# A hybrid attention kernel: squares of u behind the additions to k, weights read back in 256 KB parts, copies at the end moved

## The chip, the cores and the metric

The kernel runs on one core of a Trainium2 chip, in float32. The time is that of the device from start to end of one execution, in microseconds (us), as the median of several runs. A profile of one execution shows what each engine did: TensorE (PE, with its weight loads as PEld), VectorE (DVE), ScalarE (ACT), GpSimd (POOL), and SyncE (SP), which here issues DMAs.

## The reference, cut to what matters

Four layers with residuals over x of shape (2, 2048, 256): a gated scan, a feed-forward layer (FFN), an attention without softmax, and the FFN once more.

```
x = x + scan(layernorm(x));   x = x + ffn(layernorm(x))
x = x + hla(layernorm(x));    x = x + ffn(layernorm(x))

ffn(x): h = gelu(x @ ternary(W1).T + b1);  h @ ternary(W2).T + b2
hla(x), 16 heads of 64, step by step over t:
    G += k_t (k_t C);  S += k_t k_t^T;  C += q_t v_t^T
    o_t = q_t (S C - G)
    out @ W_o
```

The change lies in hla and in the way from it to the last FFN.

## The kernel before

**Attention in steps.** The 2048 positions of each of the two sequences are cut into 16 chunks of 128. A step `s` of the loop (L982, 32 steps, NS = 32) is one chunk `n = s // 2` of sequence `b = s % 2`; an even step is called `first` in the code. `more` is true while a further pair of chunks has still to be projected (s below 30). The chunk form of the recurrence needs, in each step: u = q S from the states before the chunk (`inter`, L835) plus the masked products of q and k inside the chunk (`products`, `intra`); the copy of u to SBUF (`evict`, L865, tile uT); the addition of k k^T to the states S and of u v^T to the states M (`update`, L874); and, one or two steps later, o = q M with the masked products of q and u, and the projection by W_o (`outward`, L899).

**The projections q, k, v** of a pair of chunks are done by seven products in place of eight (class `Seven`, L728). `go(i)` issues one product of PE and what follows it: a copy by ACT into the result (for 1, 5, 6, 4) or an addition by DVE (0, 3, 7). Products 1, 6, 7 and 4 share the PSUM bank X. So product 4 of k cannot start before the addition of product 7 has read that bank. In even steps k of the next pair is done, in odd steps q and v.

**Transposes through DRAM.** k and u are also needed transposed. DVE transposes squares of 32 x 32 into the tile sq (`turn_squares`, L914: skT for k by `keys_out`, suN for u by `units_out`), SP stores it to DRAM with one DMA of 512 KB (dkT, duN), then loads it in another order with four DMAs of 128 KB (`turn_rows`, L924: rkT, ruN), and ACT copies it to its place (`turn_end`, L935, tiles kT and uN; `units_end`, L948, for u). `update(s - 1, "uN", "vN", "M")` reads uN, `products(s, "kT", "p1")` reads kT. Only the last step's uN is made by PE (`units`, L952).

**PSUM.** Eight banks in three rings: four under "ps", two under "uT", two under "oT"; each request takes the next bank of its ring. The banks of `inter(s, "S", "uT")` are those of the ring "uT", and so is the bank X of k and of the last FFN's first products.

**Order.** PE, DVE, ACT and POOL run in the order in which the code issues their instructions (`manual_schedule`), so a line that is moved moves its instruction on its engine. SP issues DMAs in order too, and one that waits holds those behind it. DMAs issued by `nc.scalar.dma_start` stand in ACT's order.

**The last FFN.** Its weights, made ternary and combined for the seven products, were stored to DRAM by `ffn_weights_away` (w1 and w2 of 1 MB each, w1_s and w2_t3 of 768 KB each), since SBUF is needed for the attention. `ffn_weights_back` (L341) loads them into the room of wk and wv once these are read for the last time, by one DMA each:

```
            if s == NS - 4:
                last.weights("w1")
            elif s == NS - 3:
                last.weights("w2")
```

The class `Last` (L1129) does the first block of the last FFN beside the last two steps of the attention: `stats` and `rows` its norm, `turned` the transposes, `fill` the products of its first layer (generator `ffn_in`, with `apart=True`: the order p2, p1, p5, p6, p7, p3, p4 for each half), `out` those of its second. In the steps 30 and 31 `fill` stands where `k.go`, `q.go` and `v.go` stood before.

The functions that the change touches:

Of the kernel before, what the change touches and what calls it, by code (L numbers as in the profile page):

```python
# [17 lines left out]
FP = mybir.dt.float32  # L18
# [5 lines left out]
B, T, D = 2, 2048, 256  # L24
# [19 lines left out]
def kernel(  # L44
# [15 lines left out]
    nc = tc.nc  # L60
# [3 lines left out]
    const = ctx.enter_context(tc.tile_pool(name="const", bufs=1))  # L64
# [18 lines left out]
    wk = const.tile([P, ND, H * DK], FP, tag="wk", name="wk")  # L83
# [93 lines left out]
    def norm_rows(pool, cs, stats, xn=None, **kw):  # L177
        mv, rs, nb = stats
        if xn is None:
            xn = pool.tile([P, len(cs), D], FP, tag="xn", name=f"xn{cs[0]}", **kw)  # L180
        for c, g in enumerate(cs):
            if nb is None:
                nc.vector.tensor_scalar(
                    xn[:, c, :], x_sb[:, g, :], mv[:, c, 0:1], rs[:, c : c + 1],
                    ALU.subtract, ALU.mult,
                )
            else:
                nc.scalar.activation(  # L188
                    xn[:, c, :], x_sb[:, g, :], AF.Identity,
                    bias=nb[:, c : c + 1], scale=rs[:, c : c + 1],  # L190
                )
        return xn
# [145 lines left out]
            kept[nm] = dram.tile(w.shape, FP, tag=f"d{nm}", name=f"d{nm}")  # L338
            nc.sync.dma_start(out=kept[nm], in_=w)

    def ffn_weights_back(nm, tag):  # L341

        w = const.tile(kept[nm].shape, FP, tag=tag, name=f"{nm}_back")
        nc.scalar.dma_start(out=w, in_=kept[nm])
        return w

# [182 lines left out]
    def run(steps, n=None):  # L531
        for _ in steps if n is None else zip(range(n), steps):
            pass
# [169 lines left out]
    def attention(keep, pool, state, last):  # L703
# [241 lines left out]
        def units_out(s):  # L945
            turn_squares(s, "uN", d[s]["uT"].rearrange("f q (b i) -> f b q i", b=NQ))

        def units_end(s):  # L948
            turn_end(s, "uN")
            d[s]["uN"] = d[s]["uN"].rearrange("p a e -> p (a e)")  # L950
# [31 lines left out]
        for s in range(NS):  # L982
            first, n = s % 2 == 0, s // 2
            more = n + 1 < CPB
            inter(s, "S", "uT")
            products(s, "kT", "p1")
            if first and n + 2 < CPB:
                stats = norm_stats(norm_pool, pair(n + 2), bias=True)
            elif s == NS - 4:
                last.stats()  # L990
            elif s == NS - 2:
                last.second_stats()
            if s == 0:
                v.go(4)
                pairs[1] = norm_turned(norm_pool, pair(1), xn, bufs=1)
                pair_sums(1)
            if s % 2 == 1 and more:
                q, v = Seven(n + 1, "qT", "uT"), Seven(n + 1, "vN", "oT")
            if s == 1:
                q.go(2)  # L1000
                v.go(2)
                keys_out(s + 1)
            elif s % 2 == 1 and s + 1 < NS:
                keys_out(s + 1)
            if s == 2:
                k = Seven(n + 1, "kN", "uT")
                k.go(2)
            if first and s > 0:
                units_end(s - 1)
            if s >= 3:  # L1010
                outward(s - 3, 1)
            intra(s, "S", "kN", "p1", "uT")
            if s >= 2:
                intra(s - 2, "M", "vN", "p2", "oT")
            if s + 1 < NS:
                turn_rows(s + 1, "kT")
            evict(s, "uT")
            if not more:
                if s >= 2:
                    evict(s - 2, "oT")  # L1020
                last.begin(first)
                fill = last.fill
                fill(2)
                if not first:
                    units_end(s - 1)
                    units(s)
                fill(2)
            elif first:
                if s != 2:
                    k = Seven(n + 1, "kN", "uT")  # L1030
                    k.go(2)
                k.go(1)
                if s >= 2:
                    evict(s - 2, "oT")
                k.go(0, 5)
            else:
                if s >= 2:
                    evict(s - 2, "oT", dve)
                units_end(s - 1)
                units_out(s)  # L1040
                turn_rows(s, "uN")
                if s > 1:
                    q.go(2)
                    v.go(2)
                q.go(1)
                v.go(1)
                q.go(0, 5)
                v.go(0, 5)
                q.go(6)
                v.go(6)  # L1050
            if s == NS - 4:
                last.rows()
            elif s == NS - 1:
                last.second_rows()
            if s + 1 < NS:
                update(s + 1, "kN", "kN", "S")
            if s >= 1:
                update(s - 1, "uN", "vN", "M")
            if s == NS - 1:
                update(s, "uN", "vN", "M")  # L1060
            elif first:
                units_out(s)
            if not more:
                fill(2)
            elif first:
                k.go(6, 3, 7)
            else:
                v.go(7)
                q.go(7)
                v.go(3, 4)  # L1070
                q.go(3)
            if s + 1 < NS:
                turn_end(s + 1, "kT")
            if s >= 1:
                inter(s - 1, "M", "oT")
                products(s - 1, "uT", "p2")
            if not more:
                fill(1)
            elif first:
                k.go(4)  # L1080
                if n + 2 < CPB:
                    xn = norm_rows(norm_pool, pair(n + 2), stats)
            else:
                q.go(4)
            if not first and s + 2 < NS:
                keys_out(s + 2)
            if first:
                turn_rows(s, "uN")
            if not first and n + 2 < CPB:
                pairs[n + 2] = norm_turned(norm_pool, pair(n + 2), xn, bufs=1)  # L1090
                pair_sums(n + 2)
            elif s == NS - 3:
                last.turned()
            if s == NS - 4:
                last.weights("w1")
            elif s == NS - 3:
                last.weights("w2")
            if s >= 2:
                outward(s - 2, 0)
        last.out()  # L1100
# [16 lines left out]
    def pair(n):  # L1117
        return [b * CPB + n for b in range(B)]
# [10 lines left out]
    class Last:  # L1129
# [28 lines left out]
            self.rhs = ffn_rows(None, self.g0, xnT, [ts[:, i, :] for i in range(4)])  # L1158
            ffn_bias(self.g0)

        def weights(self, nm):
            nonlocal w1, w1_s, w2, w2_t3
            if nm == "w1":
                w1, w1_s = ffn_weights_back("w1", "wk"), ffn_weights_back("w1_s", "wk_t")
            else:
                w2, w2_t3 = ffn_weights_back("w2", "wv"), ffn_weights_back("w2_t3", "wv_t")

        def begin(self, first):
            if first:
# [110 lines left out]
```

## Time and profile before

| | us |
|---|---|
| median of 3 runs | 1244.42 (1243.24 to 1245.93) |
| the profiled execution: its time | 1245.38 |
| its span, first to last instruction | 1243.6 |
| PE busy | 1220.3 |
| DVE busy | 751.0 |
| ACT busy | 587.8 |
| POOL busy | 217.3 |

The attention runs from about 311 to 1053 us of the span. A line of a wait table reads: the engine and what it was about to do, the releaser, then the total in us, how often, and the longest. A line of the timeline reads: start, length, engine, line, operation, out<-in with shapes and count, and in brackets the idle time before it and what ended that. A line of the windows has the stretch, its length, the busy time of PE, PEld, DVE, ACT and POOL with counts of instructions, the clock granted to PE, the busy share of the 16 DMA engines, and GB/s. "Issue" is time in which an engine waited for nothing that the profile shows. ACTq and SPq are DMA issues in the order of ACT and SP.

### The profile page before, as it was taken

How to read it: one execution, taken by the hardware profiler on the slowest of the kernel's cores; microseconds unless marked ns; L12 is line 12 of the kernel's file. 1: busy time of each engine (PE TensorE's matmuls, PEld its weight loads, DVE VectorE, ACT ScalarE, POOL GpSimd, SP SyncE). 2: the span in 40 equal slices, each digit the busy share in tenths (PEclk: the TensorE clock that was granted, in tenths of full speed). 3: DMA queues.
4: the chain of work that ended last, by engine and by line, in shares of the span. 5: the costliest groups of instructions: out<-in, count | busy, mean ns of one | idle time of the engine just before them, and what ended most of it. 6: DMA issues, size and time to landing. Idle time of an engine off the chain costs nothing.

```text
span 1243.6 us, 46457 instructions
## 1 busy us (share of the span) xinstructions
PE 1220.3 (98%) x21244; PEld 978.1 (79%) x21244; DVE 751.0 (60%) x1261; ACT 587.8 (47%) x960; POOL 217.3 (17%) x363
## 2 busy tenths in 40 slices
PE   9999999999989999999999999999999989999998
PEld 6588777999567777777778777777777779999998
DVE  7965664665566566556656655666666544556654
ACT  4355544543455454454544545455454453354542
POOL 3743133322100100010000010000001110322220
PEclk9999999999999999999999999999999999999999
DMA  9210000000243233223323323322332530000001
GB/s 324 103 60 1 1 1 1 1 2 1 70 119 107 87 104 104 87 88 105 101 92 110 108 80 105 104 88 88 114 112 80 165 102 3 26 26 18 18 18 34
DMA packets 59555, 91.98 MB, mean 74 GB/s; under 512 B 5952, under 2 KB 49216, under 8 KB 58848
## 3 DMA queue, kind: packets, MB, share of 16 engines
q1 hardware_dynamic: 58272, 84.96, 20.6%
q10 hardware_dynamic: 1008, 3.93, 1.0%
q8 instruction: 166, 2.72, 0.9%
q0 software_dynamic: 80, 0.14, 0.1%
q14 instruction: 29, 0.24, 0.1%
HBM read 48.11 MB, written 40.89 MB: 72 GB/s over the span
## 4 chain that ended last, share of the span: by engine, by line
PE 89%; DVE 5%; issue 3%; ACT 1%; DMA 1%; POOL 0%; SPq 0%; DVEq 0%; ACTq 0%; POOLq 0%
PE ox L481 9%; PE hy L905 9%; PE hx L390 9%; PE pq L272 6%; PE hqT_X L768 5%; PE hvN_X L773 5%; PE oz L481 5%; PE hz L390 4%; PE hp L827 4%; PE hkN_X L773 3%; PE huT L858 3%; PE huT L844 3%; PE hS L884 3%; PE hoT L858 3%; PE oy L481 2%
## 5 line engine op out<-in xcount | busy, mean ns | idle before, releaser
L833 DVE TENSOR_TENSOR p<-hp,mask 128x512 f32<-128x512 f32 x128 | 82.3, 685 | 114.1 <-PE hp L827 114.1
L905 PE MATMUL hy<-wo,oT 128*128 128x256 f32 x512 | 123.6, 385 | 0.0
L905 PEld LDWEIGHTS hy<-wo,oT 128*128 128x128 f32 x512 | 93.6, 190 | 18.9 <-issue 6.7
L725 POOL TENSOR_TENSOR S<-xnT 128x128 f32<-128x128 f32 x32 | 14.7, 461 | 529.0 <-ACT xnT L205 511.4
L402 ACT ACTIVATE hT<-hT,b_sb 128x256 f32<-128x256 f32 x192 | 85.4, 501 | 36.9 <-DVE hT L434 35.4
L869 ACT COPY uT<-huT 128x512 f32<-128x512 f32 x32 | 18.7, 585 | 146.7 <-PE huT L858 146.7
L272 PE MATMUL pq<-xnT,wqkva 128*128 128x512 f32 (+1 forms) x216 | 84.9, 547 | 0.7 <-ACT xnT L216 0.3
L894 DVE TENSOR_TENSOR S<-S,hS 128x512 f32<-128x512 f32 x60 | 41.3, 688 | 58.0 <-PE hS L884 54.6
L188 ACT ACTIVATE xn<-x_sb,nb,rs 128x256 f32<-128x256 f32 x124 | 64.8, 593 | 16.4 <-POOL nb L174 16.4
L272 PEld LDWEIGHTS pq<-xnT,wqkva 128*128 128x128 f32 x216 | 40.0, 190 | 37.8 <-issue 34.7
L939 ACT COPY kT<-rkT 128x1024 f32<-128x1024 f32 x32 | 66.6, 2080 | 2.3 <-DMA rkT<-dkT 2.3
L939 ACT COPY uN<-ruN 128x1024 f32<-128x1024 f32 x31 | 64.5, 2080 | 3.0 <-DMA ruN<-duN 2.3
L919 DVE STREAM_TRANSPOSE skT<-kN 128x1024 f32<-128x1024 f32 x32 | 65.5, 2048 | 0.0
L919 DVE STREAM_TRANSPOSE suN<-uT 128x1024 f32<-128x1024 f32 x31 | 63.7, 2054 | 2.0 <-ACT uT L871 1.6
L487 DVE TENSOR_TENSOR x_sb<-x_sb,ox 128x256 f32<-128x256 f32 x64 | 26.8, 419 | 63.0 <-PE ox L481 63.0
L408 ACT COPY hT<-hx 128x512 f32<-128x512 f32 x32 | 18.7, 585 | 92.0 <-PE hx L390 92.0
L156 DVE BATCH_NORM_STATS2 st<-x_sb 128x6 f32<-128x256 f32 x128 | 51.4, 402 | 2.9 <-DMA x_sb<-in_x_dram 2.5
L884 PEld LDWEIGHTS hS<-kN 64*64 64x64 f32 x1984 | 32.7, 134 | 23.8 <-issue 23.8
L367 POOL TENSOR_TENSOR xT<-xnT 128x256 f32<-128x256 f32 x15 | 10.9, 726 | 223.6 <-ACT xnT L218 223.6
L804 ACT COPY vN<-hvN_X 128x512 f32<-128x512 f32 x16 | 9.4, 586 | 80.0 <-PE hvN_X L773 80.0
L218 ACT COPY xnT<-pt 128x512 f32<-128x512 f32 x32 | 17.2, 590 | 58.4 <-PE pt L212 50.7
L858 PEld LDWEIGHTS huT<-p,kN 64*64 64x64 f32 x2048 | 34.3, 134 | 13.2 <-issue 7.0
(243 smaller groups left out, 2894.9 us busy)
## 6 DMA issues: line engine op xcount, KB each, us to landing
dkT<-skT SPq DMA_DIRECT2D x32, 512.0 KB, 3.1
rkT<-dkT SPq DMA_DIRECT2D x128, 128.0 KB, 3.0
duN<-suN SPq DMA_DIRECT2D x31, 512.0 KB, 3.5
ruN<-duN SPq DMA_DIRECT2D x124, 128.0 KB, 3.2
out_dram<-x_sb SPq DMA_DIRECT2D x16, 256.0 KB, 2.1
x_sb<-in_x_dram SPq DMA_DIRECT2D x7, 512.0 KB, 8.9
dw<-w SPq DMA_DIRECT2D x2, 1024.0 KB, 3.9
w_back<-dw ACTq DMA_DIRECT2D x2, 1024.0 KB, 6.0
```

The lines of the kernel that those rows point to most:

```text
L188: nc.scalar.activation(xn[:, c, :], x_sb[:, g, :], AF.Identity, bias=nb[:, c : c + 1], scale=rs[:, c : c + 1],)
L272: nc.tensor.matmul(pq[:, :nt], lhsT=wqkva[:, d, col : col + P], rhs=xnT[:, d, :], start=(d == 0), stop=(d == ND - 1),)
L390: nc.tensor.matmul(at[a][:, j, :], lhsT=A[:, f * P : (f + 1) * P], rhs=Bm, start=(new and j == 0), stop=True, skip_group_check=True,)
L402: nc.scalar.activation(out, out if src is None else src[:, j, :], AF.Gelu, bias=b1_sb[:, f : f + 1])
L481: nc.tensor.matmul(banks[name][:, c, :], lhsT=A[f // 2][:, f % 2, c * P : (c + 1) * P], rhs=Bm[:, f, :], start=(new and c == 0 and f == 0) ...
L773: nc.tensor.matmul(to, lhsT=self.A[i], rhs=self.B[i], start=new, stop=True, skip_group_check=True)
L833: nc.vector.tensor_tensor(d[s][nm][:, h], banks[h], mask8, ALU.mult)
L858: nc.tensor.matmul(banks[c][halves[h ^ c], p, :], lhsT=d[s][nat][halves[c], feats(h, p)], rhs=d[s][pm][halves[c], h, p, :], start=(d[s][su ...
L884: nc.tensor.matmul(banks[c][halves[h], p, :], lhsT=d[s][left][halves[c], feats(h, p)], rhs=d[s][right][halves[c], feats(h, p)], start=True ...
L905: nc.tensor.matmul(py, lhsT=d[s]["oT"][:, p, :], rhs=wo[:, p, :], start=(p == 0), stop=(p == NPR - 1),)
L919: nc.vector.transpose(sq.rearrange("p b j q -> p b q j"), src)
L939: act(t, d[s]["r" + nm].rearrange("p t q -> p q t"))
```

## The change

Four things are moved. In even steps `units_out(s)` goes behind the rest of k's products, so that DVE does the two additions to k (L778) first and the squares suN after them. The weights come back in parts of 256 KB (512 columns of 128 partitions): `weights` only sets up a generator, and `last.part()` issues one part of it at four places of every step from step 28 on; what is left of the first group is issued at the end of step 29 by `part(None)`. The last norm's rows for the first block (`last.rows`) go from ahead of the state updates of step 28 to behind the last product of k. In the last two steps the copies of ACT move: kT of step 31 goes ahead of `fill(2)` in step 30, and uN of step 30 goes to the start of step 31, ahead of `evict(31, "uT")`; `units_out(30)` goes behind `fill(2)`. PE's instructions and their order stay as they are, and so do SP's and POOL's.

```diff
-    def ffn_weights_back(nm, tag):
-        w = const.tile(kept[nm].shape, FP, tag=tag, name=f"{nm}_back")
-        nc.scalar.dma_start(out=w, in_=kept[nm])
-        return w
+    def ffn_weights_back(w):
+        for nm, t in w.items():
+            flat = "p c e -> p (c e)" if len(t.shape) == 3 else "p c f e -> p (c f e)"
+            t, k = t.rearrange(flat), kept[nm].rearrange(flat)
+            for c in range(0, t.shape[1], 2 * D):
+                nc.scalar.dma_start(out=t[:, c : c + 2 * D], in_=k[:, c : c + 2 * D])
+                yield
...
-            if first and s > 0:
+            if s > 0 and (first or not more):
                 units_end(s - 1)
+            last.part()
             if s >= 3:
                 outward(s - 3, 1)
...
                 fill(2)
                 if not first:
-                    units_end(s - 1)
                     units(s)
                 fill(2)
...
-            if s == NS - 4:
-                last.rows()
-            elif s == NS - 1:
+            last.part()
+            if s == NS - 1:
                 last.second_rows()
             if s + 1 < NS:
                 update(s + 1, "kN", "kN", "S")
...
             if s == NS - 1:
                 update(s, "uN", "vN", "M")
-            elif first:
-                units_out(s)
+            if first and not more:
+                turn_end(s + 1, "kT")
             if not more:
                 fill(2)
             elif first:
                 k.go(6, 3, 7)
...
-            if s + 1 < NS:
+            last.part()
+            if first:
+                units_out(s)
+            if more:
                 turn_end(s + 1, "kT")
...
             elif first:
                 k.go(4)
                 if n + 2 < CPB:
                     xn = norm_rows(norm_pool, pair(n + 2), stats)
+                else:
+                    last.rows()
...
             if s == NS - 4:
-                last.weights("w1")
+                last.weights(True)
             elif s == NS - 3:
-                last.weights("w2")
+                last.part(None)
+                last.weights(False)
+            last.part()
...
-        def weights(self, nm):
+        def weights(self, one):
             nonlocal w1, w1_s, w2, w2_t3
-            if nm == "w1":
-                w1, w1_s = ffn_weights_back("w1", "wk"), ffn_weights_back("w1_s", "wk_t")
+            pairs = (("w1", "wk"), ("w1_s", "wk_t")) if one else (("w2", "wv"), ("w2_t3", "wv_t"))
+            w = {nm: const.tile(kept[nm].shape, FP, tag=tag, name=f"{nm}_back") for nm, tag in pairs}
+            if one:
+                w1, w1_s = w.values()
             else:
-                w2, w2_t3 = ffn_weights_back("w2", "wv"), ffn_weights_back("w2_t3", "wv_t")
+                w2, w2_t3 = w.values()
+            self.parts = ffn_weights_back(w)
+
+        def part(self, n=1):
+            if hasattr(self, "parts"):
+                run(self.parts, n)
```

## The prediction

> **What bounds the kernel now.** I read the page's first two parts, then who TensorE (PE) waited for, then the timeline around each of those waits, and last the granted clock and DMA share in short windows.
>
> ```profile
> PE 1220.3 (98%) x21244; PEld 978.1 (79%) x21244; DVE 751.0 (60%) x1261; ACT 587.8 (47%) x960; POOL 217.3 (17%) x363
> ```
>
> PE is busy for 1220.3 of 1243.6 us. The order and number of its instructions does not change, so all that the change can win lies in the other 23 us and in stretches at half clock. The waits of PE (us in total, times, longest):
>
> ```profile
> PE hkN_X L773 <- DVE kN L778: 4.9, 13, 2.1
> PE hoT L858 <- issue: 2.5, 1, 2.5
> PE huT L844 <- ACT hT L402: 1.5, 1, 1.5
> PE hx L390 <- issue: 1.2, 1, 1.2
> ...
> PE hM L884 <- ACT uN L939: 0.8, 1, 0.8
> ...
> PE hkN_X L773 <- ACT kN L795: 0.6, 1, 0.6
> ```
>
> These six are 11.5 us, and each lies where the change works. The first is one wait of 2.1 us in step 0 and twelve of 0.23 us in the even steps. The timeline of one of those, step 8:
>
> ```profile
> 515.02 2.07 DVE L919 STREAM_TRANSPOSE suN<-uT 128x1024 f32<-128x1024 f32 x1
> ...
> 516.90 1.11 PE L827 MATMUL hp<-qT,uT 64*64 64x64 f32 x64
> 516.92 0.69 DVE L778 TENSOR_TENSOR kN<-kN,hkN_Z 128x512 f32<-128x512 f32 x1
> ...
> 517.52 0.68 DVE L778 TENSOR_TENSOR kN<-kN,hkN_X 128x512 f32<-128x512 f32 x1
> 518.11 1.29 DVE L833 TENSOR_TENSOR p<-hp,mask 128x512 f32<-128x512 f32 x2
> 518.26 1.12 PE L773 MATMUL hkN_X<-wk_t,xnT 128*128 128x512 f32 x2 [0.24 <-DVE kN L778]
> ```
>
> The reader sees the squares of u (suN, 2.07 us) ahead of the two additions to k; PE's last product for k waits for the second addition. Then the windows behind the 2.5 us "issue" wait (the columns end with PEclk, DMA share, GB/s), and the issues ahead of it:
>
> ```profile
> 961.41 0.37 ACTq L344 DMA_DIRECT2D w_back<-dw  x1
> 961.81 0.72 ACTq L344 DMA_DIRECT2D w_s_back<-dw_s  x1
> ```
>
> ```profile
> 968.00:970.00 2.00, 0.23 (x16) 0.10 (x5) 0.67 (x2) 1.74 (x3) 0.00 (x0) 1.00 1.05 279
> 970.00:972.00 2.00, 1.28 (x48) 1.28 (x52) 0.00 (x0) 0.00 (x0) 0.00 (x0) 0.64 0.91 284
> 972.00:974.00 2.00, 2.00 (x29) 1.88 (x22) 1.41 (x3) 1.73 (x1) 0.00 (x0) 0.51 0.04 16
> ```
>
> PE stands still while the DMA engines are full of weights, and then runs at half clock: 2 x 0.36 + 2 x 0.49 = 1.7 us lost besides the 2.5. Last, step 30's end:
>
> ```profile
> 1011.75 2.02 ACT L939 COPY kT<-rkT 128x1024 f32<-128x1024 f32 x1
> ...
> 1013.68 0.82 ACT L402 ACTIVATE hT<-hx,b_sb 128x256 f32<-128x256 f32 x2
> 1014.55 1.16 PE L844 MATMUL huT<-qT,S 64*64 64x64 f32 x64 [1.48 <-ACT hT L402]
> ```
>
> The last Gelu stands behind the copy of kT, and PE waits for the bank that it reads.
>
> **The change part by part.**
>
> *A. Squares behind the additions, steps 2 to 26.* From the start of hp to that of hkN_X is 1.36 us here (516.90 to 518.26); in step 28, where no such wait stands, it is 1.04 (959.20 to 960.24). Saved: 0.32 x 12 = 3.8 us (by the waits alone 2.8). In the new order DVE's addition of M ends at 515.11, the first addition to k runs to 515.8, the second waits for PE's product (514.88 + 1.10) and ends near 516.8, well before PE wants it at 518.0. The squares then run from 516.8 to 518.9, 1.8 us later than before. Behind them on DVE: the masks of p go from 518.11 to 518.9 and end at 520.2; PE reads p at 525.97, and hp first uses a bank of theirs again at 522.02, so 1.8 us of cover remain. On SP: the 512 KB store duN and the four loads ruN move by 1.8 us; the loads are then issued by 524.9 (523.09 before), before the next store dkT can go (526.47). On ACT: the copy uN stood at 527.99; the last load was issued at 522.7 and took at least 2.9 us, so 525.6, now 527.4, and PE and ACT are 0.3 earlier: no wait. The tightest pair is step 26: 922.1 + 3.0 = 925.1 for a copy at 925.63, now 1.6 us late. Behind that copy stand ACT's copies of q and v; the first (529.96, 0.58 us) frees a bank that PE wants at 532.37: 1.8 us of cover. So nothing is paid, by a small margin. A: -3.8.
>
> *B. Step 0.* The wait is 2.12 us (PE starts at 344.83), and the windows after it give clocks 0.96, 0.50, 0.50, 0.50, 0.84: another 1.7 us. New: the second addition waits for PE (341.60 + 1.10), ends near 343.5; PE starts 1.3 earlier with 0.85 of waiting left. Waits of 0.80 (322.70) and 1.48 (1014.55) were followed by clock 1.00, so the half clock goes too: -3.0. Here a rule of the Trainium skill ("TensorE: Matmul & The Clock Gate", Why this matters for your kernels) speaks against me: only idle gaps over about 3 us between matmuls throttle. By it the half clock would not come from waits of 2.12 and 2.49 us and would stay: D would be -1.7, and the whole sum -5.8 instead of -6.9. The trace has half clock right after these two and after no shorter wait, so I take the rows. But the units pay: the squares end at 345.5 and not at 343.66; the loads landed 8.2 us behind (347.7 + 4.2 = 351.9), so now at 353.7, while ACT, 3.0 us earlier, is ready for the copy at 351.4. It ends at 355.8, the copy of q at 356.4; PE wants that bank at 354.0 and waits 2.4 us. So -0.6, or +1.1 if that wait halves the clock. B: 0.
>
> *C. Rows of the last norm behind k.* The 0.60 us wait in step 28 goes. The four rows (2.07 us) move into the 6.18 us in which ACT idled before 968.17. C: -0.6.
>
> *D. Weights in parts, first group.* 1.75 MB went out at 961.4, beside 0.5 MB of ruN, at 280 to 400 GB/s: 8 us full. Now two parts (0.5 MB) go behind the rows, near 964, beside the same ruN, itself 1.9 us later: about 3.5 us full. "Issue" names no releaser; queue 8 fetched 2.72 MB of instructions in 166 packets, and a late fetch fits. The ends are 0 (a fetch caught as before) and 2.49 + 1.7 = 4.2; since the other "issue" waits of the attention, beside its everyday traffic, are 1.0 us at most, I take two thirds. D: -2.8.
>
> *E. Second group.* At 991 1.75 MB go; now the three parts of w1_s left over and one of w2, 1.0 MB, with the others in steps 30 and 31. Of the 1.23 us wait at 1000.27, 0 to 1.2 goes; I take 0.7. E: -0.7.
>
> *F. Ten more issues on ACT*, each 0.33 to 0.72 us by its rows: 3 to 7 us of an engine that is idle for 5 us or so where they stand (5.19 ahead of the v copies, 4.64 ahead of the Gelus of step 30). The skill's "DMA: Bandwidth & Descriptors" asks, under Bandwidth, for transfers of 1 MiB or more, and fits, under Anatomy of one DMA, 2.0 us plus the bytes at 436 GB/s to each: by that estimate a part costs 2.6 us, and four, if one followed the other from 991.5, would land at 1002, just when w1_s is first read (1002.0), so up to 1 us of wait. The rows speak against that: 128 KB loads land in 3.0 us with four under way together. F: 0.
>
> *G. Steps 30 and 31.* Gains: kT's copy goes into ACT's idle time (1005.5 to 1010.1), so 1.48 goes; additions ahead of the squares, 0.22; uN's copy earlier, 0.76. Together 2.5. Paid: the squares of step 30 end at 1011.0 and not at 1009.58; loads landed 7.8 us behind (1014.6 + 2.8), with parts of w2 beside them say 8.4: 1019.4. ACT now has that copy ahead of uT's: 2.06, an issue 0.35, the first uT copy 0.58: 1022.4. PE wants that bank at 1019.8 (1021.49 - 1.7): 2.6 us, then about 0.9 us more for the copy of hT behind it. Ends: -2.5 (loads early) to +2.7 (half clock too). G: +1.0.
>
> Sum: -3.8 + 0 - 0.6 - 2.8 - 0.7 + 0 + 1.0 = -6.9 us. The profiled execution took 1245.38 with a span of 1243.6, 1.8 us lying around it: the new span would be 1236.7, its time 1238.5. The median of the runs is 1.0 below the profiled one, so 1244.4 - 6.9 = 1237.5.
>
> **The rivals.**
>
> *All waits go and nothing comes back.* -3.8 - 3.0 - 0.6 - 4.2 - 1.2 - 2.5 = -15.3: 1229. For it: each wait is named and its releaser moved. Against: the u chain is 8 us long and is started later in the same edit.
>
> *Only the small waits go.* The fetch is caught again (D, E 0), and both late copies halve the clock (B +1.1, G +2.7): -0.6 in all, 1243.8, no change. For it: both late waits, 2.4 and 2.6 us, lie in the range that halved the clock.
>
> *The units hold ACT in every odd step (slower).* Place: the copy uN ahead of the copies of q and v. The shift of 2.1 us eats the 2.4 us in front of the copy; 1.8 us more lie behind it. If store and loads also take longer in their new place (from squares to landing they took 8.5 us in step 8 and 10.4 in step 26), every us past that is paid 13 times. It outweighs the 6.9 us when each pair loses 0.5; at 1.2 a pair it is +15.6 - 6.9 = +8.7: 1253. Against: only step 26 stands near the limit.
>
> **How the numbers follow.** My forecast has 0.64, the first rival 0.17, the second 0.12, the third 0.07. My own case runs from 1233 to 1242; the range 1231 to 1243.5 takes in the second rival's better half and the first's upper end. 0.2% is 2.5 us, about what a measurement of this kernel can tell from no change (three runs lay within 2.7). Faster takes the first two cases, less a little: 0.80; same 0.12; slower 0.08.
>
> **What would show it.** A: no wait of hkN_X for DVE in even steps but step 0, and masks at 0.8 us after hp. B: hqT_X waiting in step 1 for ACT, about 2 us. C: xn behind the last copy of k. D: the DMA share full for about 4 us instead of 8, a shorter "issue" wait at hoT, clock 1.00. G: huT without its wait, and instead hx waiting near 2 us for ACT in step 31. I am wrong if odd steps show PE waiting for ACT's copies of q or v, or if the "issue" waits move elsewhere and add up to as much.

## The result, and the profile after

The changed kernel takes 1238.97 us in the median of 6 runs (1236.43 to 1241.06); the kernel before, on the same chip, 1245.26 (1243.24 to 1246.89). The ratio is 0.9949, with a 95% interval of 0.9934 to 0.9965: 6.3 us faster, against 6.9 forecast. The profiled execution took 1239.59 us with a span of 1237.8.

PE's row of the profile, and then whom PE waited for (us in total, times, longest), both of the changed kernel:

```profile
PE 1217.9 (98%) x21244; PEld 976.1 (79%) x21244; DVE 753.2 (61%) x1261; ACT 588.0 (48%) x960; POOL 217.9 (18%) x363
```

```profile
PE hqT_X L772 <- ACT qT L791: 4.4, 1, 4.4
PE hx L394 <- ACT uT L873: 2.3, 1, 2.3
PE hM L888 <- issue: 1.4, 1, 1.4
PE huT L862 <- issue: 1.2, 3, 0.5
PE hp L831 <- ACT kT L943: 1.2, 1, 1.2
...
PE hkN_X L777 <- DVE kN L782: 0.8, 1, 0.8
...
PE hx L394 <- ACT hT L412: 0.4, 1, 0.4
PE hx L394 <- issue: 0.4, 1, 0.4
```

The thirteen waits of hkN_X for DVE have become one of 0.8 us in step 0. The stall of 2.5 us at hoT, huT's wait for ACT and hM's for uN are gone. On top stand two waits for ACT that were not there before; both were forecast, at 2.4 and 2.6 us. The wait of hM for "issue", 0.9 us before, is in steps 2 and 3. That of hp for kT stands ahead of step 0's first mask, where the change moves nothing, and is 0 to 1.4 us from trace to trace.

An even step in the new order, step 8 in the timeline of the changed kernel:

```profile
519.69 0.69 DVE L782 TENSOR_TENSOR kN<-kN,hkN_X 128x512 f32<-128x512 f32 x1 [0.18 <-PE hkN_X L777]
...
520.30 2.05 DVE L923 STREAM_TRANSPOSE suN<-uT 128x1024 f32<-128x1024 f32 x1
520.57 1.11 PE L831 MATMUL hp<-qT,uT 64*64 64x64 f32 x64
...
521.61 1.13 PE L777 MATMUL hkN_X<-wk_t,xnT 128*128 128x512 f32 x2
522.21 1.25 DVE L837 TENSOR_TENSOR p<-hp,mask 128x512 f32<-128x512 f32 x2
```

hkN_X follows hp with no bracket for a wait, 1.04 us after hp's start where it was 1.36. The masks of p pay, and nobody waits for them.

Step 0 and step 1, same view:

```profile
343.84 2.04 DVE L923 STREAM_TRANSPOSE suN<-uT 128x1024 f32<-128x1024 f32 x1
...
345.91 0.34 SPq L925 DMA_DIRECT2D duN<-suN  x1
...
350.98 1.73 SPq L933 DMA_DIRECT2D ruN<-duN  x4
...
356.46 2.02 ACT L943 COPY uN<-ruN 128x1024 f32<-128x1024 f32 x1 [4.49 <-DMA ruN<-duN]
...
358.39 0.58 ACT L791 COPY qT<-hqT_X 128x512 f32<-128x512 f32 x1
...
359.02 2.08 PE L772 MATMUL hqT_X<-S,wq_t 128*128 128x128 f32 x8 [4.42 <-ACT qT L791]
```

ACT stands 4.49 us before the copy of uN, because the loads land only at 356.4; behind that copy stands the copy of q, and PE waits for it. The eight products that follow take 2.08 us in place of 1.16. The granted clock, third from the end of each window's row, says why:

```profile
358.00:360.00 2.00, 0.97 (x4) 0.98 (x5) 0.99 (x2) 2.00 (x5) 0.00 (x0) 0.63 0.48 154
360.00:362.00 2.00, 2.00 (x8) 1.23 (x6) 0.29 (x1) 1.02 (x2) 0.00 (x0) 0.52 1.03 236
```

Where PE had stood still behind step 28 (the windows end with clock, DMA share, GB/s):

```profile
960.00:962.00 2.00, 2.00 (x58) 1.56 (x61) 0.26 (x1) 2.00 (x5) 0.00 (x0) 1.00 0.97 291
962.00:964.00 2.00, 2.00 (x94) 1.85 (x85) 0.65 (x2) 0.14 (x1) 0.00 (x0) 1.00 0.83 258
964.00:966.00 2.00, 2.00 (x62) 1.59 (x64) 2.00 (x3) 0.00 (x0) 0.00 (x0) 1.00 0.73 192
966.00:968.00 2.00, 2.00 (x94) 1.93 (x84) 1.55 (x3) 1.62 (x3) 0.00 (x0) 1.00 0.48 169
```

PE is busy throughout, at full clock. And the end of step 30:

```profile
1012.75 2.02 ACT L943 COPY uN<-ruN 128x1024 f32<-128x1024 f32 x1 [7.63 <-DMA ruN<-duN]
...
1014.68 0.58 ACT L873 COPY uT<-huT 128x512 f32<-128x512 f32 x1
...
1015.31 1.13 PE L394 MATMUL hx<-xnT,w_back 128*128 128x256 f32 x4 [2.31 <-ACT uT L873]
```

uT's copy could have gone before; it stands behind uN's, whose loads are late.

Where time comes and goes is read from the starts of the same masks of p (DVE, p<-hp) in the trace of each kernel. The columns, in us of one profiled execution: from the first mask of all, in step 0, to the first of step 1; on to the second of step 1; from the first of step 4 to the second of step 27; then from the second of step 28 to the second of 29, of 30 and of 31. (From step 1 on, each step masks first the products with k, then those with u.) (The kernels e1 to e12 are introduced below.)

| kernel | step 0 | step 1 | steps 4 to 27 | behind 28 | behind 29 | 30 to 31 |
|---|---|---|---|---|---|---|
| before | 16.5 | 18.2 | 525.4 | 28.8 | 21.5 | 21.4 |
| changed | 13.6 | 24.0 | 520.4 | 24.1 | 20.7 | 22.3 |
| e1 step 0 old | 16.5 | 18.2 | 520.5 | 24.1 | 20.7 | 24.0 |
| e2 uN of 30 old | 13.6 | 23.9 | 520.2 | 25.2 | 20.7 | 19.6 |
| e3 squares alone | 15.0 | 18.2 | 519.3 | 29.4 | 21.6 | 21.4 |
| e4 weights whole | 13.6 | 25.0 | 520.8 | 26.4 | 21.4 | 21.2 |
| e5 parts at once | 13.6 | 19.8 | 521.9 | 26.4 | 22.4 | 22.3 |
| e6 uN of 0 behind q, v | 13.6 | 18.7 | 520.0 | 24.1 | 20.7 | 23.2 |
| e7 = e6 and e2 | 13.6 | 18.9 | 520.5 | 25.4 | 20.7 | 20.1 |
| e8 parts alone | 15.0 | 18.2 | 525.3 | 27.3 | 21.6 | 21.4 |
| e9 step 28 old | 13.6 | 23.8 | 521.1 | 25.1 | 20.7 | 25.1 |
| e10 = e7, parts later | 13.6 | 18.6 | 521.4 | 24.3 | 21.7 | 19.5 |
| e11 = e8, parts later | 16.5 | 18.2 | 524.8 | 24.6 | 20.7 | 21.4 |
| e12 = e1 and e2 | 16.3 | 18.4 | 520.8 | 24.7 | 20.7 | 19.5 |

Between the first two rows lie -2.9, +5.8, -5.0, -4.7, -0.8 and +0.9; what is left (0.5 ahead of the attention, 0.6 in steps 2 and 3, -0.3 in step 28's products of k) makes -5.9 of it, and the spans differ by 5.8.

### The profile page after: what moved, and what is told of

The parts are those of the page before. It is cut to its first block, busy times and chain, and to the rows that moved or that the text cites. A ratio compares the mean times of both kernels' runs of the same rounds, so it can differ in the third digit from the quotient of the medians.

```text
span 1237.8 us, 46471 instructions
## 1 busy us (share of the span) xinstructions
PE 1217.9 (98%) x21244; PEld 976.1 (79%) x21244; DVE 753.2 (61%) x1261; ACT 588.0 (48%) x960; POOL 217.9 (18%) x363
## 3 DMA queue, kind: packets, MB, share of 16 engines
q8 instruction: 166, 2.72, 0.9%
## 4 chain that ended last, share of the span: by engine, by line
PE 95%; DMA 2%; DVE 1%; ACT 1%; issue 1%; SPq 0%; POOL 0%; ACTq 0%; DVEq 0%; POOLq 0%
PE ox L485 9%; PE hy L909 9%; PE hx L394 9%; PE pq L272 6%; PE hkN_X L777 5%; PE hqT_X L772 5%; PE hp L831 5%; PE oz L485 5%; PE hvN_X L777 4%; PE hz L394 4%; PE hoT L848 3%; PE hS L888 3%; PE huT L862 3%; PE huT L848 3%; PE hM L888 2%; PE hoT L862 2%
## 5 line engine op out<-in xcount | busy, mean ns | idle before, releaser
L909 PEld LDWEIGHTS hy<-wo,oT 128*128 128x128 f32 x512 | 93.6, 190 | 18.9 <-issue 6.7
L272 PEld LDWEIGHTS pq<-xnT,wqkva 128*128 128x128 f32 x216 | 40.0, 190 | 37.3 <-issue 34.7
L782 DVE TENSOR_TENSOR kN<-kN,hkN_Y 128x512 f32<-128x512 f32 x16 | 11.0, 688 | 57.0 <-ACT kN L791 57.0
```

What stands on the lines that cost most here:

```text
L272: nc.tensor.matmul(pq[:, :nt], lhsT=wqkva[:, d, col : col + P], rhs=xnT[:, d, :], start=(d == 0), stop=(d == ND - 1),)
L909: nc.tensor.matmul(py, lhsT=d[s]["oT"][:, p, :], rhs=wo[:, p, :], start=(p == 0), stop=(p == NPR - 1),)
```

## The experiments

Ratios are against the kernel before on the same chip, with their 95% intervals.

**Step 0's squares at their old place (e1).**

```
@@ of the changed kernel, ahead of k.go(6, 3, 7)
+            if s == 0:
+                units_out(s)
...
-            if first:
+            if first and s > 0:
                 units_out(s)
```

> The changed kernel, but with step 0's squares, store and loads of u at their old place, ahead of the additions to k; every other step as changed. My theory is that the new place costs more in step 0 and 1 than it saves there (traces: 2.85 us won in step 0, 5.82 lost in step 1, net +2.97): the loads land at 8 us behind the squares instead of 10.6, the wait of PE for ACT's copy of q in step 1 (4.4 us, and the half clock behind it) goes, and the wait of 2.1 us for the second addition in step 0 with its half clock comes back. So about 1236, 3.0 us under the changed kernel's 1239 and 9 under the kernel before. Rival 1: the long wait in step 1 is an accident of that one profiled execution (a store that landed late), and the place is worth the 0 that I had predicted: then 1239 and, in the profile, squares to landing at 10 us from the old place too. Rival 2: the order in step 0 is worth its full 3.0 us gain: then 1242.

Measured: 1236.68, ratio 0.9929 [0.9916, 0.9943], 2.3 us under the changed kernel, with intervals that overlap. In the table, steps 0 and 1 fall from 37.6 to 34.7 together, the 3.0 expected. So the edit of step 0, taken alone, was a loss in the traces. From squares to landing the trace shows 8.25 us here, as before (8.17), and 10.56 in the changed kernel. The first rival is partly right too: in the other kernels with the late place this chain took 10.3, 10.3, 7.8, 10.0, 10.3, 9.0 and 10.0 us (e2, e4, e5, e6, e7, e9, e10), and in e5, with the same code in step 1, PE waited 1.6 us and not 4.4. It is the rule, with exceptions.

The store ahead of these loads accounts for the 2.4 us between the two. Step 0 of the kernel before (343.6 to 346.3) and of the changed one (345.9 to 350.9):

```profile
q1 hardware_dynamic: 144, 0.52, 47.3%
...
duN<-suN SPq DMA_DIRECT2D x1, 512.0 KB, 2.6
```

```profile
q1 hardware_dynamic: 144, 0.52, 26.2%
q8 instruction: 1, 0.02, 1.2%
...
duN<-suN SPq DMA_DIRECT2D x1, 512.0 KB, 5.0
```

From the old place (before, e1, e3, e8, e11, e12) the store landed 2.6 us after its issue, all its 144 packets starting within 1.45 us of the first. From the new one it landed after 3.3 to 5.0 us in all eight traces, with 3 to 9 packets starting late. In each of these eight, and in none of the six, one packet of PE's instructions (queue q8, see e8) moved while the store was under way. That they meet there is shown; which holds up which is not, for in e2, e4 and e5 the late packets begin to show before the instruction packet starts.

Some of the gain is lost at the end: the wait of hx for ACT grew to 3.6 us, with half clock behind it.

```profile
PE hx L394 <- ACT uT L873: 3.6, 1, 3.6
```

**Step 31's copy of uN at its old place (e2).**

```
-            if s > 0 and (first or not more):
+            if s > 0 and first:
                 units_end(s - 1)
...
                 if not first:
+                    units_end(s - 1)
                     units(s)
```

> The changed kernel, but step 31's copy of uN is issued at its old place, behind the fill and ahead of the units of step 31, so that ACT takes the first copy of uT before it. My theory: the wait of hx for ACT's copy of uT (2.3 us) and the one for hT behind it (0.4) both come from that copy standing first; they go, and at most 0.8 us of a wait of hM for uN comes back: 1236.3 to 1237.1, that is 1.9 to 2.7 us under the changed kernel's 1239. Rival: the copy was only the last in a chain that is late anyway (the loads of uN land at 1012.7 in the trace), and hM then waits for uN by the same 2.3 us: no gain, 1239.

Measured: 1234.24, ratio 0.9904 [0.9889, 0.9919]. The table has -2.7 for steps 30 and 31, as expected; the wait of hM for uN that comes back is 0.8:

```profile
PE hM L888 <- ACT uN L943: 0.8, 1, 0.8
```

The median fell by more, 4.7. That fits the rows of e1, e6 and e9, with the changed kernel's code there: 24.0, 23.2 and 25.1 in place of 22.3. Their waits of hx are 3.6, 2.5 and 3.0 us and have half clock behind them; the profiled execution of the changed kernel escaped it.

**The squares alone (e3).**

```
@@ of the kernel before
-            elif first:
+            elif first and (s == 0 or s >= NS - 4):
                 units_out(s)
...
                 q.go(3)
+            if first and 0 < s < NS - 4:
+                units_out(s)
```

> The kernel before with one edit: squares, store and loads of u go behind the additions to k in steps 2 to 26 (steps 0 and 28 stay as they were, nothing else is changed). My theory: 12 pairs of steps gain 0.30 us each, 3.6 in all, and PE shows no wait for ACT's copies in odd steps: 3.6 us under the kernel before, about 1241.6. Rival: part of the gain that the two traces show between steps 4 and 28 (5.0 us) belongs to this edit through fewer small waits on instruction issue, then 5.0 under the kernel before, 1240.2. Rival: the later loads cost what the additions win, then no difference.

Measured: 1240.05, ratio 0.9953 [0.994, 0.9967], 5.1 us under the kernel before. The second figure was met. Steps 4 to 27 take 524.8 to 525.4 in the three traces of the old order and 519.3 to 521.9 in the eleven of the new one: 4.5 in the mean. Pair by pair the masks show 0.3 (3.7 in all). The rest is products of huT, hoT and hqT_Y that are held up now and then with no releaser named: beyond the shortest steps they add 4.0 to 4.7 us in the old order and 1.9 to 4.7 in the new one. They differ as much between traces of one order, so this part is not shown to come from the edit. Nor is all of e3's 5.1 its own: in its profiled execution, the median one, step 0 escaped its half clock with the old code, which is worth 1.5.

**Weights whole (e4), and parts all at once (e5).**

```
@@ e4
-            for c in range(0, t.shape[1], 2 * D):
-                nc.scalar.dma_start(out=t[:, c : c + 2 * D], in_=k[:, c : c + 2 * D])
-                yield
+            nc.scalar.dma_start(out=t, in_=k)
+            yield
@@ e4 and e5
             elif s == NS - 3:
-                last.part(None)
                 last.weights(False)
-            last.part()
+            last.part(None)
```

> The changed kernel, but the FFN's weights come back in whole transfers at their old places (two behind step 28, two behind step 29) and not in parts of 256 KB spread over six places; all other edits stay. My theory: the stall of PE behind step 28 (2.5 us, by the profile waiting for nothing but issue) and the half clock behind it return, and the 1.2 us one at hx behind step 29 too: 4.2 + 0.8 = 5.0 us over the changed kernel's 1239, so 1244. Rival: the stall was a chance meeting of one fetch with the transfers, and with the other edits having moved everything by some us it does not return: 1239, clock 1.00 throughout.

> The changed kernel, with the weights still in parts of 256 KB, but all seven parts of a group go out together, behind step 28 and behind step 29. It tells smaller transfers from spread ones. My theory: what matters is how long the DMA engines are full when an instruction page of PE has to come, so parts that go out together are as bad as whole weights: a stall of PE near 2 us at hoT behind step 28, half clock behind it or not, DMA share full for about 8 us; times near those of the kernel with whole weights (1244.3, spread from 1236 to 1247), 4 to 5 us over the changed kernel's 1239. Rival: small transfers alone let the fetch through: 1239, no such stall.

e4: 1244.29, ratio 0.998 [0.9966, 0.9994], 5.3 over the changed kernel; its 20 runs lie between 1235.88 and 1247.27, so some escape. e5: 1241.32, ratio 0.9965 [0.9952, 0.9978], 2.4 over, with intervals that overlap. In e4's trace PE is held at hoT again, 1.9 us of it behind step 28:

```profile
PE hoT L861 <- issue: 3.1, 2, 1.9
...
PE hx L393 <- issue: 1.2, 1, 1.2
```

In e5's the hold at hoT is 0.8 us and not the 2 expected, so smaller transfers help there. But the wait of hx for issue stays (1.3), and two waits of PE for ACT's copies of uT come on top (1.0): the stretches behind 28 and 29 cost 4.0 more than in the changed kernel and 0.9 more than in e4. That e5's median lies 3.0 under e4's may be step 1, which is 5.2 shorter in its trace. So in the traces it is the spreading that counts; by the medians the two are not told apart.

**Step 1's copy of uN behind four copies of q and v (e6), and both copies moved (e7).**

```
-                units_end(s - 1)
+                if s > 1:
+                    units_end(s - 1)
                 units_out(s)
...
                 v.go(0, 5)
+                if s == 1:
+                    units_end(0)
                 q.go(6)
```

> The changed kernel, with step 1's copy of uN moved on ACT from ahead of step 1's copies of q and v to behind the first four of them. Squares, store and loads of step 0 stay at their new, late place. My theory: the loads' lateness does harm only through ACT's order, since PE needs uN later than q: the wait of 4.4 us for ACT's copy of q and the half clock behind it go, and PE waits at most 1.1 us for uN at hM: 4.7 under the changed kernel's 1239, 1234.3. Rival: uN itself is late for hM by as much (3 us or more): 1239. Rival: the copies of q and v then run late for their own readers through the loss of ACT's idle time: a new wait of PE for ACT in step 1 or 2, 1236 to 1238.

> Both copies of uN moved: step 1's behind the first four copies of q and v, and step 31's back behind the fill. The two places lie 650 us apart, so the gains add, by my theory: 4.7 + 2.7 (the second measured as 2.7 in the traces of the run that moved it alone) = 7.4 under the changed kernel's 1239, 1231.6. Rival: the second gain depends on how the first shifts the loads against instruction fetches and weights, as the run with step 0's old place hints, where the wait of hx for ACT grew to 3.6 us: then anything from 1231 to 1236.

e6: 1235.56, ratio 0.9929 [0.9913, 0.9945], 3.4 of the 4.7 us expected. The loads land as late as ever (10.0 us behind the squares), and yet step 1 falls from 24.0 to 18.7:

```profile
356.03 2.06 ACT L943 COPY uN<-ruN 128x1024 f32<-128x1024 f32 x1 [0.70 <-DMA ruN<-duN]
...
358.15 1.16 PE L888 MATMUL hM<-vN,uN 64*64 64x64 f32 x64 [0.59 <-ACT uN L943]
```

The copies of q and v have used the time in which ACT stood still, and PE waits 0.59 us for uN itself. No new wait for q or v appears. e7: 1231.30 (1230.18 to 1232.61), ratio 0.9886 [0.9871, 0.99], the best of all: 7.7 under the changed kernel and 14 under the one before. The gains add.

**Parts alone (e8).** The kernel before with `ffn_weights_back`, `weights` and `part` of the changed kernel and its places of `last.part()`:

```
@@ of the kernel before
+                nc.scalar.dma_start(out=t[:, c : c + 2 * D], in_=k[:, c : c + 2 * D])
+                yield
...
-                last.weights("w1")
+                last.weights(True)
             elif s == NS - 3:
-                last.weights("w2")
+                last.part(None)
+                last.weights(False)
+            last.part()
```

> The kernel before with one edit: the weights back in parts of 256 KB at the four places, everything else as before. My theory: the stall of PE behind step 28 (2.5 us) with its half clock (1.7) and most of the 1.2 us one behind step 29 go: 5.0 us under the kernel before, 1240.2, and the granted clock is 1.00 behind step 28. Rival: the stall is a chance meeting of a fetch and transfers, with the parts as likely as with the whole: no difference, 1245. Rival: the ten more issues on ACT, here ahead of the copies of step 30, cost it what the stall gives: 1242 to 1245.

Measured: 1243.9, ratio 0.9986 [0.9978, 0.9994], only some 1.5 us. My theory fell: without the rest of the change the parts leave the stall where it was.

```profile
PE hoT L862 <- issue: 2.9, 2, 2.5
PE hx L394 <- issue: 1.7, 2, 1.5
```

In the profiled execution just the half clock behind it was missing. So what ends the stall? Queue q8 carries instructions, for which the profile counts 166 packets of 16 KB and 2.72 MB; that is 64 bytes for each of PE's 21244 products and 21244 weight loads, so they are taken to be PE's. Call such a packet an instruction page. The same one of them belongs to the stall in every kernel, and the later it starts to move, the longer PE is held. Counted from step 28's second mask of p, in the traces:

| | page moves, us behind the mask | PE held at hoT |
|---|---|---|
| changed, e1, e6, e10, e11, e12 | 4.5 to 5.1 | 0 to 0.3 |
| e2, e5, e7, e9 | 5.5 to 5.7 | 0 to 1.0 |
| before, e3, e4, e8 | 6.9 to 8.1 | 1.9 to 2.9 |

Where PE is held, it goes on 2.5 to 2.9 us after the page has begun to move. Two stretches of the DMA queues show it, of the kernel before (967.8 to 968.8) and of the changed one (963.6 to 964.6; packets, MB, share of the 16 engines):

```profile
DMA packets 98, 0.35 MB, mean 354 GB/s; under 512 B 12, under 2 KB 48, under 8 KB 97
...
q10 hardware_dynamic: 49, 0.30, 83.0%
...
q8 instruction: 1, 0.02, 6.8%
```

```profile
DMA packets 236, 0.26 MB, mean 261 GB/s; under 512 B 29, under 2 KB 202, under 8 KB 235
...
q8 instruction: 1, 0.02, 6.3%
```

In the first PE has stopped (at 968.2) and goes on at 970.72; in the second it is 1.5 us and more ahead of hoT (966.13). What the page meets differs. At 5 us behind the mask e8 has loads of u (q1) and weights (q10) moving together, 2 to 3 us into both; the kernel before has weights alone moving, between two bursts of loads; in the changed kernel the first two parts are nearly through and the loads have just begun. In e4 the loads go out late and the weights whole. There nothing but weights moved, apart from ten packets of next to no bytes, in the 3.9 us before the page's start at 966.99 (962.8 to 966.7), and PE was held for 1.9:

```profile
q10 hardware_dynamic: 224, 1.54, 101.3%
q1 hardware_dynamic: 10, 0.00, 0.1%
```

So whole weights go with a late page while hardly a byte of the loads, issued at 963.5, is moving.

**Step 28's squares at their old place (e9).**

```
@@ of the changed kernel, ahead of k.go(6, 3, 7)
+            if s == NS - 4:
+                units_out(s)
...
-            if first:
+            if first and s != NS - 4:
                 units_out(s)
```

> The changed kernel, but step 28's squares, store and loads of u stand at their old place, ahead of the additions to k; all else as changed, the spread parts of the weights too. What is open: parts alone in the old order won 1.3 us only and kept a stall of 2.5 us at hoT behind step 28, while in the changed kernel this stall is gone. In the traces of ten kernels PE resumes 2.5 to 2.9 us after the instruction page that it needs there begins to move (page at 967.84, PE at 970.72 before; page at 963.67, PE due at 966.13 and not held after). My theory: the page comes late when the loads of u (0.5 MB) go out with the first two parts; with step 28's squares early they do again, the page starts 1 to 2 us later against PE's work, and a stall of 1.5 to 2.5 us returns: 2 us over the changed kernel's 1239, 1241 (half clock behind it would add up to 1.7). Rival: the stall's size depends on the weights alone: no stall beyond 1 us, 1239. Both: up to 0.6 more where the copy of k waits.

Measured: 1238.47, ratio 0.9936 [0.9924, 0.9949] (its profiled execution was its slowest, 1243.32): the rival was right, there is no stall at hoT. But the run did not make the condition that it was meant to make. Its loads left 2.9 us behind the mask, 3.4 in the changed kernel, 1.2 in e8, and the page moved at 964.53, in time.

**Parts held back: after both copies moved (e10), and in the old order (e11).**

```
-            last.part()
+            if s != NS - 3:
+                last.part()
...
-            last.part()
+            last.part(2 if s == NS - 3 else 1)
...
-            last.part()
+            last.part(2 if s == NS - 3 else 1)
...
-            last.part()
+            if s != NS - 4:
+                last.part()
```

> The kernel with both copies of uN moved (1231.3), and the first group's parts held back: none behind step 28 and at the start of step 29, two behind step 29's copies of q and v and two behind its additions, the other three where they were. Then no weights are under way when PE needs its page behind step 28. My theory: the stall there (1.0 us in that kernel's trace) goes and nothing comes in its place: 1230.3, up to 1.3 under it. Rival: the page was held by the loads of u, not by the parts: no change. Rival: the parts meet the next pages in steps 29 and 30 and the stall moves there, or the first read of the weights waits: 1232 or more.

> The kernel before with the weights in parts only, as in the run that took 1243.9, but the first group's parts are held back: none behind step 28 and at the start of step 29, two behind step 29's copies of q and v and two behind its additions. It asks what holds PE at hoT behind step 28 in the old order. My theory: PE asks there for an instruction page, and the page moves only behind the packets that were queued before; in the old order both the loads of u and two parts are queued before PE asks, in the changed kernel the loads come later. Without the parts there only the loads (0.5 MB) are ahead: the page moves 2 us earlier, the 2.5 us stall falls under 0.8, and the time is 1.7 to 2.5 us under 1243.9: 1241.4 to 1242.2. Rival: the loads of u alone hold the page: stall 2.5 again, 1243.9. Rival: the stall goes, but the parts meet a later page: stall of 1 us or more in step 29 or at hx, 1243 to 1244.

e10: 1232.16 (1229.29 to 1234.58), ratio 0.9892 [0.9878, 0.9907], no better than e7. The stall behind 28 goes, and one of 0.8 us comes behind 29: the last rival.

```profile
PE huT L862 <- issue: 0.8, 1, 0.8
```

e11: 1239.93, ratio 0.9959 [0.9949, 0.9968], against 0.9986 in e8: 3 to 4 us better, more than expected. The stretches behind 28 and 29 are as short as in the changed kernel, and PE's wait at hoT is small (from 935 us on):

```profile
PE hoT L862 <- issue: 0.2, 1, 0.2
```

Here the loads of u move as early as in e8, and the page moves at once (4.7 us behind the mask). So the loads alone don't hold it, and parts can be had for the full 5 us by themselves, if none goes out with those loads.

**Steps 0 and 31 both undone (e12).** The edits of e1 and e2 together:

```
+            if s == 0:
+                units_out(s)
...
+            if s > 0 and first:
                 units_end(s - 1)
...
+                    units_end(s - 1)
                     units(s)
```

> The changed kernel with step 0's squares, store and loads at their old place and step 31's copy of uN back behind the fill: what is left of the change are the squares behind the additions from step 2 on, the parts, the norm's rows and kT's copy. It tells what the new place in step 0 is worth once the order on ACT does not turn it into a loss. My theory: in the kernel with both copies moved, step 0 keeps its 2.85 us gain and step 1 pays 0.8, so this kernel, which has the wait of 2.1 us and the half clock in step 0 but no wait in step 1, is about 1 to 2 us slower than that one's 1231.3: 1232.3 to 1233.3. Rival: the two orders are worth the same, 1231.3. Rival: the wait of hx for ACT, 3.6 us when step 0 alone was undone, stays: 1235.

Measured: 1233.91, ratio 0.9911 [0.9893, 0.9929], 2.6 over e7. The late squares in step 0 are worth having once ACT's order fits (the two intervals overlap by a little); the table has 32.5 us for steps 0 and 1 in e7 and 34.7 here.

## Why the prediction was right, point by point

The time was met for the right main reasons, but three sizes were off by a us or more (A, B, D), and they largely cancelled; that much of the closeness is luck.

- **A, the squares: -3.8 forecast; -5.0 in the two traces, -5.1 by e3's median.** The mechanism is as told, and the rival in which the units hold ACT in every odd step didn't come: outside step 1 no product of q or v waits for ACT's copies behind uN. The 0.32 per pair was right; the rest, hold-ups with no releaser, was not in my sum and varies from trace to trace.
- **B, step 0: 0 forecast, +3.0 measured. This is the step that failed.** The gain was sized rightly (-3.0, measured -2.9). The payment was not: "the loads landed 8.2 us behind", carried over to the new place, became 10.6. The store alone took 5.0 us to land where 2.6 had been enough before, and at the new place it meets an instruction page (e1). With it the wait was 4.4 and not 2.4 us, and the half clock, which I had kept for the upper end, came too. e1 undoes it, and e6 shows that lateness cost only through the order on ACT.
- **C, the norm's rows: -0.6 forecast.** The 0.60 us wait is gone.
- **D, first weights: -2.8 forecast, -4.2 measured**, the outer end: the whole 2.5 us and 1.7 of half clock. "A late fetch fits" was right, and taking two thirds was too careful. But the reason given, fewer us of full DMA engines, is not enough: e8 had it (4 us, 964 to 968) and kept the stall. What goes with the stall in every trace is how late the page moves, and that depends on what is under way when it is due. And the parts didn't go out behind the norm's rows near 964, but ahead of them, though they stand behind them in ACT's order:

```profile
959.59 1.15 ACTq L348 DMA_DIRECT2D w_back<-dw  x2
...
960.06 2.07 ACT L188 ACTIVATE xn<-x_sb,nb,rs 128x256 f32<-128x256 f32 x4
```

  So a DMA on ACT's queue didn't wait for work of the engine that stands ahead of it.
- **E, second weights: -0.7 forecast, -0.8 measured. F: nothing forecast, nothing seen;** two parts took 1.15 us to issue. The fit that I weighed there is given by the Trainium skill ("DMA: Bandwidth & Descriptors", Anatomy of one DMA) for DMAs that GpSimd issues, and these are ACT's: the parts took 2.7 to 6.3 us to land and not 2.6. Those of w1_s had landed by 991.65, 3.1 us before their first read.
- **G, steps 30 and 31: +1.0 forecast, +0.9 in the profiled execution,** with hx waiting 2.3 us where I had 2.6. Over the six traces with this code in place it is -0.2 (e4, whose loads landed 7.6 us behind, with no wait of hx for uT) to +3.7, 1.6 in the mean; the half clock follows in three. My "lands 8.4 us behind" is 8.6 to 10.0 in the other five.
- The rule of the Trainium skill that I weighed ("TensorE: Matmul & The Clock Gate", Why this matters for your kernels), that only gaps over about 3 us throttle, doesn't hold here, nor does mine that any wait over 2.1 does. Step 0's wait of 2.1 us was followed by half clock in before, e1, e11 and e12, and by clock 1.00 in e3 and e8, with the same code there:

```profile
346.00:348.00 2.00, 2.00 (x52) 2.00 (x56) 0.00 (x0) 1.56 (x3) 0.00 (x0) 0.50 0.17 54
```

```profile
346.00:348.00 2.00, 1.81 (x28) 1.06 (x29) 0.13 (x1) 0.65 (x2) 0.00 (x0) 1.00 0.57 234
```

The first is of the kernel before, the second of e8. Waits of 2.3 us (changed, e5) left the clock alone; those of 2.5 did so once (e8) and not twice (before, e6); all of 2.85 and more halved it. The same page, under What's actually happening, speaks of a free-running window of 3413 ns. If what counts is how a wait falls into such windows, 2 to 3 us are a matter of chance, which would fit these rows; no run here tests it. My sum by that rule was wrong too: the half clock would stay in step 0 as well, so B would be +1.1 (1.3 won, 2.4 paid), and the whole -4.7, not -5.8.

What stays open: which of the packets ahead of it hold an instruction page. Loads of u alone don't (e11), whole weights do with next to none of them moving (e4), and two parts do where the loads go out early beside them (e8) but not where they start 2 us later (changed); a run with parts alone wasn't made. Nor do these starts settle it all: in e2 and e7 loads and parts go out as in the changed kernel (3.4 and 0.6 us behind the mask), and the page still moves about 1 us later and PE is held for 0.8 and 1.0 us. For the late store of step 0, no run moved store and page apart.

## What to carry to other kernels

When a transfer is started later, look on the engine that takes delivery for what stands behind that copy in its order: move the copy behind whatever is ready earlier, and the lateness may cost nothing (e6, e7). Carry a transfer's time to a new place only with a margin, for it depends on what else is under way there. Where PE stands still for "issue" near a burst of DMA, spread the burst and keep it away from other large transfers; cutting it into smaller ones that leave together gained little here (e5).

## What the runs showed of the hardware

- An instruction page of PE (16 KB, 166 in a run) that comes while whole weights, or two parts together with early loads of u, are under way can hold PE for 1.9 to 2.9 us; PE goes on 2.5 to 2.9 us after it starts to move. The Trainium skill ("Runtime: NRT & Kernel Launch", Instruction fetch mechanics) has the same blocks of 16 KiB and says that crossing to the next is mostly hidden. It mostly is (steps 4 to 27 show 0.5 to 2.1 us of waits with no releaser in all), but not beside 1 MB or more of other transfers.
- The same store of 512 KB took 2.6 us to land in one place of step 0 (six traces) and 3.3 to 5.0 in another, 2 us later, where an instruction page was under way in all eight traces.
- One short wait of PE can cost 1.7 us of half clock or none, from execution to execution: step 0's of 2.1 us did in four of six traces. In three places it cost 3.4 (step 1 in e4 and e9, the end of step 30 in e9), behind waits of 4.2, 2.9 and 3.0 us.
